# Layer 0's first expert block inside the first stage's plan, and gathered rows turned four blocks at a time by VectorE and SBUF transfers

## Chip, core and metric

The kernel runs on one core of one Trainium2 chip. The metric is the device time of one launch in microseconds (us). Most times below are of one profiled execution; the runs that are compared are timed without a profile.

## What is computed

Two layers work on x of 4 batches x 1024 tokens x 256 features (fp32). Each layer adds a mixing part (layer 0: a form of linear attention; layer 1: a gated feed-forward net with running decay) and a mixture of 8 experts, both behind a layer norm with shifts and scales made from a condition vector. The part that the change touches is layer 0's mixture:

```python
logits = jnp.einsum('bsd,de->bse', input_emb, Wr) + br
route_w = jax.nn.softmax(logits, axis=-1)
_, topk_idx = jax.lax.top_k(route_w, TOP_K)          # 2 of 8 experts for each token
...
h = jax.nn.relu(jnp.einsum('bsd,edh->ebsh', input_emb, W1) + b1[:, None, None, :])
expert_out = jnp.einsum('ebsh,ehd->ebsd', h, W2) + b2[:, None, None, :]
return jnp.einsum('bse,ebsd->bsd', routed, expert_out)
```

with D = 256 features, H = 1024 hidden units, E = 8 experts, and 4096 tokens, so 8192 pairs of token and expert.

## The kernel before

**The first stage** (up to some 115 us of the span) does layer 0's attention part, its layer norms and the routing. Its pieces are given to a planner (`Plan`): each piece has an engine, an estimated time, the pieces it comes after, the buffers it holds and a rank; the planner runs them in a simulated time and so writes down the order of the instructions on each engine. Each engine then works through its own list in that order, and waits on semaphores. The normalised rows are stored to a table in HBM, `h_rows` (L1316), with the token's routing code beside them (L1303).

**The routing's end.** The pairs are sorted by expert into blocks of 128. `total_staged` (PE, L561 and L569) counts pairs, `close_staged` (DVE, L596 to L649) turns the counts into a list of blocks, `across` (PE, L688) spreads it over the partitions, `limits` (DVE, L699 to L714) and `list_weights` (L725 to L736) write the tables. For each block `reach` (DVE, L752), `look` (PE, L765) and `find` (DVE, L778 and L787) find which 128 rows belong to it. Block 0 needs only `begin` (L580 and L583), not the list of blocks. Small matmuls without use (`busy`, L915) keep PE at work in the gaps; PE also makes layer 1's modulation there (`pm_mod`, L1382).

**The expert loop** runs over blocks 0 to 59 (of 71; `turning` = 60) in an order written out by hand. In turn j it issues on POOL the gather of W1 for block j+1 (`weights_in`), the scatter of block j-2's values (`kept`), the gather of W2 for block j (`weights_out`) and the gather of 128 rows of block j+2 (`fetch`); both weight gathers move data only where the expert differs from that of two blocks before. PE does `hidden(j)` (L1698: 16 fp32 matmuls with W1 as weights and the turned rows as moving operand, 2 records each), then turns the rows of block j+1 (`turn_rows`, L1678: two 128x128 transposes into PSUM), looks for block j+3 (L765), and does `values(j-1)` (L1721). ACT adds the bias and rectifies (L1710). DVE copies the turned rows to SBUF (`rows_turned`, L1683), makes the addresses (`aim`, L799), finds the rows, and adds the last bias (L1732). `once(j)` puts 16 loads for layer 1 on the queue of SP, from turn 8 on; SP waits for no block between them.

**The rest.** The last expert blocks (60 to 67) and layer 1 are planned again, in stages that overlap.

The lines to know in the code below: `first_half` and `second_half` plan the first stage, the `for j in range(AHEAD)` loop the first three looks, and the `with tc.manual_schedule(engines=ORDERED | {EngineType.SP})` block is the expert loop.

Of the kernel before, what the change touches and what calls it, by code (L numbers as in the profile page):

```python
# [19 lines left out]
P = 128  # L20
B, S, D = 4, 1024, 256
NC = S // P
KD = D // P
# [9 lines left out]
ROUTER = 64  # L33
STRIP = 32
AHEAD = 3
DX = D + 2
W1ROW = KD * H + KH
W2ROW = KH * D + D
# [101 lines left out]
def adaln_d2_kernel(  # L140
# [218 lines left out]
    class Pairs:  # L359
# [222 lines left out]
            )  # L582
            nc.vector.tensor_copy(self.nth[:, 0:1], lane)  # L583

        def close_staged(self, scratch):


            J, blocks, runs, origin, up1 = self.J, self.blocks, self.runs, self.origin, self.up1
            begin2 = float(J - LATE)

            def t(shape, what, dt=F32):
                return scratch.tile(shape, dt, tag=f"g_{what}", name=f"g_{what}", bufs=1)

# [4 lines left out]
            )  # L598
            blocks_i = t([P, 2, E], "blocks_i", I32)
            nc.vector.tensor_scalar(blocks_i, whole, 7, None, ALU.logical_shift_right)  # L600
            nc.vector.tensor_copy(blocks[:, :, 1:], blocks_i)

            up = t([P, 2, E + 1], "up")
            nc.vector.tensor_tensor_scan(
# [141 lines left out]
        def reach(self, scratch, j):  # L746

            reached = scratch.tile(
                [P, self.halves, P], F16, tag="g_reached", name="g_reached", bufs=3
            )  # L750
            for h in range(self.halves):
                nc.vector.tensor_scalar(  # L752
                    reached[: self.K, h, :],
                    count16[: self.K],
                    self.limit[: self.K, h, j : j + 1],
                    None,
                    ALU.is_ge,
                )
            return reached
# [35 lines left out]
        def aim(self, scratch, xg, j):  # L795


            dest = scratch.tile([P, 1], I32, tag="g_dest", name="g_dest", bufs=8)
            nc.vector.scalar_tensor_tensor(  # L799
                dest,  # L800
                xg[:, D : D + 1],
                self.code[:, j : j + 1],
                xg[:, D + 1 : D + 2],
                ALU.not_equal,
                ALU.add,
            )
            return dest
# [96 lines left out]
    sT1 = silu_of(1, c1)  # L904
    gate_rows = pa.tile([B, 2, D], F32, name="gate_rows", bufs=1)

    plan = Plan(p1=3, p2=2, pm=3, xn1=5, h1T=2, xn2=6, h2T=2, t1=1, le=2)
    PE, ACT, DVE, POOL = "PE", "ACT", "DVE", "POOL"
    tiles = {}
# [299 lines left out]
    def second_half(b):  # L1209
# [73 lines left out]
        for gs in routed:  # L1283
            k, at = 4 * len(gs), 4 * gs[0] * B + b
            tag = (b, gs[0])

            def route(k=k, at=at, tag=tag):
                g0.route(pa, tiles["pl", tag[0], tag[1]][:, :, :E], br_sb, at, k, B)

            d = plan(  # L1290
                DVE,
                0.24 * 14 + 0.16 * 4 if k == NC else 0.22 * 14,
                route,
                after=[ready[g][0] for g in gs],
                holds=[ready[gs[-1]][1]],
                rank=rank - 0.2,
            )
            for g in gs:
                of_batch["route", b, g] = d

            def mark(k=k, at=at):
                first = at - at % B
                nc.sync.dma_start(  # L1303
                    h_rows[first * P : (first + k * B) * P, D:].rearrange(
                        "(c b p) d -> b p c d", b=B, p=P
                    )[at % B],
                    g0.meta[:, at : at + (k - 1) * B + 1 : B, :],
                )

            plan("SP", 1.0, mark, after=[d], rank=rank)  # L1310
            for g in gs:
                back, slot, key = backs[g]

                def store(g=g, key=key):
                    at = 4 * g * B * P
                    nc.sync.dma_start(  # L1316
                        h_rows[at : at + 4 * B * P, :D].rearrange(
                            "(c b p) d -> b p c d", b=B, p=P
                        )[b],
                        tiles["xn", key],  # L1320
                    )

                plan("SP", 4.0, store, after=back, holds=[slot], rank=rank)


    ps = plan.slot("p1")
# [75 lines left out]
        tiles["bases"] = g0.bases(ps_1)  # L1402

    m2 = plan(PE, 0.2, bases, after=[d], holds=[ps2], rank=-1.6)
    d = plan(DVE, 3.9, lambda: g0.close_staged(pa), after=[m], holds=[ps], rank=-1.0)
    bs = plan(
        ACT,
        0.25,
# [3 lines left out]
        rank=-1.6,  # L1412
    )
    begun = plan(DVE, 0.3, g0.begin, after=[bs], rank=-1.6)
    ps = plan.slot("p1")
    m = plan(PE, 0.4, lambda: g0.across(ps_1), after=[d], holds=[ps], rank=-1.0)
    kept_busy(1.1, [m], 30.0)
    d = plan(DVE, 1.4, lambda: g0.limits(pa), after=[m, bs], holds=[ps], rank=-1.0)
    plan(DVE, 1.2, lambda: g0.list_weights(pa), after=[d], holds=[ps], rank=-0.75)
    for j in range(AHEAD):  # L1420
        ps = plan.slot("p1")

        def reach(j=j):
# [8 lines left out]
        first = -1.0 + 0.1 * j if j else -1.6  # L1432
        r = plan(DVE, 0.5, reach, after=[d] if j else [begun], rank=first)
        m = plan(PE, 0.25, look, after=[r], holds=[ps], rank=first)
        plan(DVE, 0.6, find, after=[m], holds=[ps], rank=first if j else -0.95)
        if j < AHEAD - 1:
            kept_busy(0.7, [m], 30.0 + j)
    with tc.manual_schedule(engines=ORDERED):
# [10 lines left out]
    mods1 = [l1.tile([P, B, D], F32, name=f"mod{i}") for i in range(6)]  # L1449
    groups = [Pairs(l1, l1, "ga", 4 * B), Pairs(l1, l1, "gb", 3 * B)]  # L1450
    mod_rows1 = dram.tile([B, 6, D], F32, name="mod_rows1")
    early = ctx.enter_context(tc.tile_pool(name="early", bufs=1))
    poolF = tc.tile_pool(name="poolF", bufs=2, side="right")
    work = poolF.__enter__()
    y0 = dram.tile([2 * B * S, D], F32, name="y0")
    groups_of["g0"], values_of["g0"] = g0, y0

# [23 lines left out]
    RINGS = tuple(room1)  # L1481
    SP = "SP"
    made = {}
    home = {"yg1": early, "h1": early, "hT1": early, "tiny": early}

    def buf(kind, shape):
        return (home[kind] if kind in home else late).tile(
# [184 lines left out]
            ts.append(plan(ACT, 0.67, out_, after=[m], holds=[ps, slotT], rank=rank - 0.03))  # L1672
        return slot, slotT, hs, ts

    def turn_rows(j):
        pt = psum(ps_m, [P, KD, P], "pm_x")
        for k in range(KD):
            nc.tensor.transpose(pt[:, k, :], xgbuf[j % 4][:, k * P : (k + 1) * P], ident)  # L1678
        return pt

    def rows_turned(pt):
        xT = work.tile([P, KD, P], F32, tag="xT", name="xT", bufs=3)
        nc.vector.tensor_copy(xT, pt)  # L1683
        return xT

    def weights_in(j):
        gather(w1buf[j % 2], W1, g0.wrow[:, j : j + 1], E * P - 1)

    def weights_out(j):
        gather(w2buf[j % 2], W2, g0.wrow[:, j : j + 1], E * P - 1)  # L1690

    def hidden(j, xT, m4):
        w1 = w1buf[j % 2]
        p1 = psum(ps_1, [P, 4, P], "p1_h")
        for i in range(4):
            m = 4 * m4 + i
            for k in range(KD):
                nc.tensor.matmul(  # L1698
                    p1[:, i, :],
                    lhsT=w1[:, k * H + m * P : k * H + (m + 1) * P],  # L1700
                    rhs=xT[:, k, :],
                    start=(k == 0),
                    stop=(k == KD - 1),
                )
        return p1

    def rectified(j, hid, p1, m4):
        for i in range(4):
            m = 4 * m4 + i
            nc.scalar.activation(  # L1710
                hid[:, m, :],
                p1[:, i, :],
                AF.Relu,
                bias=w1buf[j % 2][:, KD * H + m : KD * H + m + 1],
            )

    def values(j, hid):
        w2 = w2buf[j % 2]
        p2 = psum(ps_2, [P, D], "p2_y")
        for m in range(KH):  # L1720
            nc.tensor.matmul(  # L1721
                p2,
                lhsT=hid[:, m, :],
                rhs=w2[:, m * D : (m + 1) * D],
                start=(m == 0),
                stop=(m == KH - 1),
            )
        return p2

    def biased(j, p2):  # L1730
        y = work.tile([P, D], F32, tag="y", name="y", bufs=3)
        nc.vector.tensor_tensor(y, p2, w2buf[j % 2][:, KH * D :], ALU.add)  # L1732
        return y

    dests, ys0 = {}, {}

    def aimed(j):
        dests[j] = g0.aim(work, xgbuf[j % 4], j)

    def kept(j):  # L1740
        put("g0", dests[j], ys0[j])

    def new_hidden():
        return work.tile([P, KH, P], F32, tag="hid", name="hid")


    loads = []
    for k in range(KD):
        loads += [(a[:, k, :], w[k * P : (k + 1) * P, :]) for a, w in ((a0, fw0), (a2, fw2))]
# [24 lines left out]
            nc.sync.dma_start(*loads[j - 8])  # L1774

    with tc.manual_schedule(engines=ORDERED | {EngineType.SP}):
        for j in range(2):
            g0.fetch(xgbuf[j], h_rows, j)
        xT, hid = rows_turned(turn_rows(0)), None
        aimed(0)  # L1780
        for j in range(turning):

# [2 lines left out]
                kept(j - 2)  # L1785
            if j:
                weights_out(j)
            g0.fetch(xgbuf[(j + 2) % 4], h_rows, j + 2)
            reached = g0.reach(work, j + AHEAD)
            new = new_hidden()  # L1790
            for m4 in range(2):
                rectified(j, new, hidden(j, xT, m4), m4)

            xT = rows_turned(turn_rows(j + 1))
            aimed(j + 1)
            g0.find(work, g0.look(ps_m, reached), j + AHEAD)
            if j:
                ys0[j - 1] = biased(j - 1, values(j - 1, hid))
            hid = new
            once(j)  # L1800


    plan = Plan(rings=RINGS, **room1)
    of_block = {}

# [762 lines left out]
```

## Time and profile before

| | |
|---|---|
| timed without a profile | 1121.61 us median of 3 runs (1121.43 to 1122.06) |
| the profiled execution: its own time, and its span | 1141.97 us, 1140.2 us |
| PE busy | 1086.3 us, 95% of the span |
| DVE, ACT, POOL busy | 592.0 us, 428.6 us, 422.5 us |
| start of block 0's `hidden`, and of the last matmul of an expert block (67) | 115.0 us, 622.0 us |

How to read the profile: PE is the matmul part of TensorE and PEld its weight loads, which lie beside matmuls; DVE is VectorE, ACT is ScalarE, POOL is GpSimd (it issues gathers), SP is SyncE (it issues plain transfers). A line of the timeline has start, length, engine, source line, operation, tiles written<-read, shapes, and count; what stands in brackets is the idle time ahead of it and what ended it. In a table of stretches each row has the length, the busy time and count of each engine, the granted clock, the mean busy share of the 16 DMA engines, and GB/s.

### The profile page before, as it was taken

To read this page: it belongs to the slowest core of one execution; us is meant where nothing else is said; L and a number is where in the kernel's file an instruction comes from. 1 tells how busy PE (TensorE), PEld (TensorE's weight loads), DVE (VectorE), ACT (ScalarE), POOL (GpSimd) and SP (SyncE) were. 2 spreads that over 40 slices of the span, in tenths; PEclk is the share of its full clock that TensorE was granted. 3 is DMA by queue.
4 is the path that set the end of the run, shared out by engine and by line. 5 is a ranking of instruction groups with operands and counts; after the bars stand their busy time and mean duration, and the time that the engine had idled before them with its cause. 6 is when DMAs were issued, how large, how long until landed. Compare 5 with 4: busy or idle time off the path is not lost. (4 is left out here: it accounts for less than half of the span.)

```text
span 1140.2 us, 18501 instructions
## 1 busy us (share of the span) xinstructions
PE 1086.3 (95%) x6238; PEld 847.0 (74%) x6238; DVE 592.0 (52%) x2308; ACT 428.6 (38%) x1164; POOL 422.5 (37%) x483
## 2 busy tenths in 40 slices
PE   8998999999999999999999999999999999899883
PEld 5894999999999999999988466566576575547641
DVE  7787232222222222222274788975776445888456
ACT  5976333322333323233343343432434235333421
POOL 1000455555555555555543011010044233616452
PEclk8999999999999999999999999999999999999996
DMA  9414549242422415151260312100024223323532
GB/s 321 174 31 103 191 156 302 100 153 75 154 78 75 150 39 192 33 193 40 70 223 27 96 34 83 39 10 19 19 62 129 75 82 103 102 88 107 155 118 93
DMA packets 77693, 122.38 MB, mean 107 GB/s; under 512 B 27340, under 2 KB 57301, under 8 KB 72990
## 3 DMA queue, kind: packets, MB, share of 16 engines
q0 software_dynamic: 31872, 69.68, 19.5%
q1 hardware_dynamic: 44622, 49.92, 13.3%
q10 hardware_dynamic: 1104, 1.58, 0.4%
q8 instruction: 52, 0.85, 0.3%
q14 instruction: 43, 0.35, 0.1%
HBM read 205.25 MB, written 30.22 MB: 207 GB/s over the span
## 5 line engine op out<-in xcount | busy, mean ns | idle before, releaser
L1710 ACT ACTIVATE hid<-p_h,w 128x128 f32<-128x128 f32 x544 | 154.8, 368 | 323.5 <-issue 251.9
L1698 PEld LDWEIGHTS p_h<-xT,w 128*128 128x128 f32 x2176 | 253.2, 192 | 7.2 <-DVE xT L1683 1.9
L1698 PE MATMUL p_h<-xT,w 128*128 128x128 f32 x2176 | 254.7, 275 | 3.1 <-DVE xT L1683 2.7
L1721 PE MATMUL p_y<-w,hid 128*128 128x256 f32 x1088 | 249.0, 382 | 0.2 <-issue 0.2
L2007 PE MATMUL p_u<-hT,a 128*128 128x512 f32 x512 | 232.0, 596 | 2.9 <-ACT hf L2019 1.4
L1721 PEld LDWEIGHTS p_y<-w,hid 128*128 128x128 f32 x1088 | 201.6, 190 | 25.1 <-DMA w<-in_W,g_wrow 0.4
L2007 PEld LDWEIGHTS p_u<-hT,a 128*128 128x128 f32 x512 | 93.5, 190 | 100.5 <-issue 89.7
L347 POOL DMA_INDIRECT w<-in_W,g_wrow x134 | 135.1, 1008 | 77.4 <-ACT hid L1710 46.7
L1683 DVE COPY xT<-pm_x 128x256 f32<-128x256 f32 x68 | 28.8, 424 | 187.0 <-PE pm_x L1678 134.4
L812 POOL DMA_INDIRECT y<-y,g_dest x68 | 69.5, 1022 | 143.5 <-DVE g_reached L752 108.4
L2055 PE MATMUL p_f<-a,hf 128*128 128x256 f32 x512 | 116.7, 380 | 2.0 <-DVE step L2096 1.0
L1732 DVE TENSOR_TENSOR y<-p_y,w 128x256 f32<-128x256 f32 x68 | 28.9, 425 | 166.9 <-PE p_y L1721 160.7
L2055 PEld LDWEIGHTS p_f<-a,hf 128*128 128x128 f32 x512 | 95.9, 190 | 20.8 <-issue 5.9
L347 POOL DMA_INDIRECT xg<-h_rows,g_row x68 | 66.7, 980 | 120.4 <-DVE g_row L787 98.9
L2103 POOL TENSOR_TENSOR x_sb<-x_sb,step 128x256 f32<-128x256 f32 x32 | 24.9, 778 | 205.8 <-DVE step L2096 153.6
L2315 PE MATMUL p_e<-ew,xT 128*128 x280 | 71.5, 386 | 0.8 <-ACT y L2325 0.8
L2019 ACT ACTIVATE hf<-p_u,decay 128x512 f32<-128x512 f32 x56 | 38.2, 685 | 74.9 <-PE p_u L2007 63.5
L347 POOL DMA_INDIRECT xg<-ga_rows,ga_row x39 | 37.3, 956 | 54.1 <-DVE g_hits L778 19.3
L2315 PEld LDWEIGHTS p_e<-ew,xT 128*128 128x128 f32 x280 | 49.0, 190 | 11.0 <-issue 3.8
L2023 DVE SCALAR_TENSOR_TENSOR hf<-p_u,decay,hf 128x512 f32<-128x512 f32 x56 | 41.9, 748 | 25.7 <-PE p_u L2007 14.3
L1618 DVE TENSOR_TENSOR h<-h,mod 128x256 f32<-128x256 f32 x128 | 51.6, 425 | 6.8 <-ACT h L1608 4.1
L2325 ACT COPY y<-p_e 128x256 f32<-128x256 f32 x70 | 26.1, 373 | 51.4 <-PE p_e L2315 19.2
(371 smaller groups left out, 1259.1 us busy)
## 6 DMA issues: line engine op xcount, KB each, us to landing
yg<-y SPq DMA_DIRECT2D x32, 256.0 KB
ga_y<-y SPq DMA_DIRECT2D x39, 128.0 KB
x_sb<-in_x SPq DMA_DIRECT2D x8, 512.0 KB
h_rows<-xn SPq DMA_DIRECT2D x8, 512.0 KB
gb_y<-y SPq DMA_DIRECT2D x31, 128.0 KB
out_x<-x_sb SPq DMA_DIRECT2D x7, 512.0 KB
a<-in_fw SPq DMA_DIRECT2D x6, 512.0 KB
mod<-mod_rows SPq DMA_DIRECT2D x6, 512.0 KB
```

The source lines that it names most:

```text
L347: return nc.gpsimd.indirect_dma_start(out=dst, out_offset=None, in_=table, in_offset=bass.IndirectOffsetOnAxis(ap=index, axis=0), bounds_c ...
L812: nc.gpsimd.indirect_dma_start(out=table, out_offset=bass.IndirectOffsetOnAxis(ap=dest, axis=0), in_=y, in_offset=None, bounds_check=2 * s ...
L1618: nc.vector.tensor_tensor(h, h, mods1[(sc, sh)[i]][:, b, :], (ALU.mult, ALU.add)[i])
L1698: nc.tensor.matmul(p1[:, i, :], lhsT=w1[:, k * H + m * P : k * H + (m + 1) * P], rhs=xT[:, k, :], start=(k == 0), stop=(k == KD - 1),)
L1710: nc.scalar.activation(hid[:, m, :], p1[:, i, :], AF.Relu, bias=w1buf[j % 2][:, KD * H + m : KD * H + m + 1],)
L1721: nc.tensor.matmul(p2, lhsT=hid[:, m, :], rhs=w2[:, m * D : (m + 1) * D], start=(m == 0), stop=(m == KH - 1),)
L1732: nc.vector.tensor_tensor(y, p2, w2buf[j % 2][:, KH * D :], ALU.add)
L2007: nc.tensor.matmul(pu, lhsT=a[:, k, m * P : (m + 1) * P], rhs=made["n1", c, "hT"][:, k, :, :], start=(k == 0), stop=(k == KD - 1),)
L2019: nc.scalar.activation(made[key, m], made[key, m, 0], AF.Silu, scale=decays[c])
L2023: nc.vector.scalar_tensor_tensor(h, made[key, m, 1], decays[c], h, ALU.mult, ALU.mult)
L2055: nc.tensor.matmul(made[key, "p2", b], lhsT=made[key, m][:, b * P : (b + 1) * P], rhs=a1[:, m, :], start=(m == 0), stop=(m == KH - 1),)
L2315: nc.tensor.matmul(made[key, "p2"], lhsT=made[key, "xT"][:, k, :], rhs=ew_flat[:, bass.ds(made[key, "at"] + k * D, D)], start=(k == 0), st ...
```

## The change

It has two parts.

1. Block 0's row gather, turning, `hidden` and `values` become pieces of the first stage's plan (`first_block`), and the copy of its turned rows is done by ACT. The first three instructions of `close_staged` become `whole_blocks`; the rest of it, `across`, `limits` and `list_weights` are entered in the plan after block 0's look and find. Block 1's gather is planned too.
2. Blocks 12 to 59 come in groups of four (a quad). Their rows are gathered up to eight blocks ahead into a buffer of four blocks (`xgquad`). At the end of turn j (j = 8, 12, ..., 52) `quad_turned(j + 4)` has DVE turn 32x32 squares, two instructions of 128x512 values, and SP issue 16 transfers from SBUF to SBUF of 32 partitions x 256 values, which put the squares in their places. The moving operand of `hidden` is then four runs of 32 columns that lie 256 values apart. PE's two transposes and DVE's copy are gone for these 48 blocks. The looks run up to ten blocks ahead, two in each of turns 2 to 8. W1's rows are laid out differently by the host, so the rows are turned with a step of two; for blocks 0 to 11 and 60 to 67 this step is in the weight load of PE's transposes. The buffers `early` for the start of layer 1 are taken after the loop, in place of the quads' buffers.

```diff
-            dest = scratch.tile([P, 1], I32, tag="g_dest", name="g_dest", bufs=8)
+            dest = scratch.tile([P, 1], I32, tag="g_dest", name="g_dest", bufs=16)
...
-    d = plan(DVE, 3.9, lambda: g0.close_staged(pa), after=[m], holds=[ps], rank=-1.0)
+    whole = plan(DVE, 0.45, lambda: g0.whole_blocks(pa), after=[m], holds=[ps], rank=-1.0)
...
+    def quad_turned(j):
+        rows = xgquad[j // QUAD % 2]
+        square = quads.tile([P, P // SQ, KD, QUAD, SQ], F32, tag="square", name="square", bufs=1)
+        for k in range(KD):
+            nc.vector.transpose(
+                square[:, :, k, :, :].rearrange("p m b s -> p b m s"),
+                rows[:, :, k:D:KD].rearrange("p b (m f) -> p b m f", f=SQ),
+            )
+        xT = quads.tile([P, P // SQ, KD, QUAD, SQ], F32, tag="xTq", name="xTq")
+        for q in range(P // SQ):
+            for m in range(P // SQ):
+                nc.sync.dma_start(
+                    xT[m * SQ : (m + 1) * SQ, q, :, :, :], square[q * SQ : (q + 1) * SQ, m, :, :, :]
+                )
+        for b in range(QUAD):
+            turned_quads[j + b] = [xT[:, :, k, b, :] for k in range(KD)]
+            dests[j + b] = g0.aim(work, rows[:, b, :], j + b)
...
+    def first_block(found):
+        slots = [plan.slot("xn1") for _ in range(2)]
+        kept0 = tiles["first"] = {}
+        rows = plan(
+            POOL, 1.0, lambda: g0.fetch(xgbuf[0], h_rows, 0), after=[found, *stores], rank=-1.6, lag=1.9
+        )
...
+        m = plan(PE, 0.35, turn, after=[rows], holds=[ps, *slots], rank=-1.5)
+        h = plan(ACT, 0.45, lambda: nc.scalar.copy(kept0["xT"], kept0["pt"]), after=[m], holds=[ps, *slots], rank=-1.5)
...
     for j in range(AHEAD):
+        if j == 1:
+            closed = plan(
+                DVE, 3.5, lambda: g0.close_staged(pa), after=[whole, found], rank=-1.0
+            )
...
-        plan(DVE, 0.6, find, after=[m], holds=[ps], rank=first if j else -0.95)
+        found = plan(DVE, 0.6, find, after=[m], holds=[ps], rank=first)
+        if j == 0:
+            first_block(found)
...
-        for j in range(2):
-            g0.fetch(xgbuf[j], h_rows, j)
-        xT, hid = rows_turned(turn_rows(0)), None
+        looks = {0: (3,), 1: (4,)} | {j: (j + 3, j + 10) for j in range(2, 9)}
+        fetches = {j: (j + 2,) for j in range(4)} | {j: (j + 2, j + 8) for j in range(4, 10)}
+        xT, hid = None, None
...
-            xT = rows_turned(turn_rows(j + 1))
-            aimed(j + 1)
-            g0.find(work, g0.look(ps_m, reached), j + AHEAD)
-            if j:
+            if in_quads(j + 1):
+                xT = turned_quads.pop(j + 1)
+            else:
+                xT = rows_turned(turn_rows(j + 1))
+                aimed(j + 1)
+            for r, hit in zip(sought, reached):
+                g0.find(work, g0.look(ps_m, hit), r)
+            if j == 1:
+                ys0[0] = biased(0, tiles["first"]["p2"])
+            elif j:
                 ys0[j - 1] = biased(j - 1, values(j - 1, hid))
+            if j % QUAD == 0 and in_quads(j + QUAD):
+                quad_turned(j + QUAD)
```

## The prediction

> **What bounds the kernel now.** I read the page first, for who is busy and when; then the table of stretches, for the stages apart; then the timeline of PE inside one turn of the expert loop, and of PE and DVE where the first stage ends.
>
> ```profile
> span 1140.2 us, 18501 instructions
> ...
> PE 1086.3 (95%) x6238; PEld 847.0 (74%) x6238; DVE 592.0 (52%) x2308; ACT 428.6 (38%) x1164; POOL 422.5 (37%) x483
> ```
>
> ```profile
> 241.84:249.25 7.41, 7.41 (x55) 6.99 (x53) 1.73 (x8) 2.28 (x8) 3.99 (x5) 1.00 0.54 179
> 115.00:560.00 445.00, 444.59 (x3131) 419.32 (x3132) 109.29 (x503) 139.10 (x485) 238.65 (x239) 1.00 0.38 125
> 650.00:1140.00 490.00, 452.62 (x1802) 281.26 (x1800) 341.54 (x1235) 171.22 (x412) 145.61 (x158) 0.98 0.26 78
> ```
>
> Of the 445 us of the loop PE is without work for 0.41 us, at full clock. DVE has work for a quarter of it, POOL for a little over half. So a microsecond taken from PE's list in the loop is a microsecond off the span, and DVE, ACT, POOL and the DMA engines (0.38 busy) have room.
>
> One turn of the loop on PE:
>
> ```profile
> 245.68 3.73 PE L1698 MATMUL p_h<-xT,w 128*128 128x128 f32 x32
> 249.25 0.38 PE L1678 MATMUL pm_x<-ident,xg 128*128 128x128 f32 x2
> 249.47 0.28 PE L765 MATMUL pm_counts<-g_more,g_reached 128*128 128x129 f16 x2
> 249.59 3.67 PE L1721 MATMUL p_y<-w,hid 128*128 128x256 f32 x16
> 253.09 3.73 PE L1698 MATMUL p_h<-xT,w 128*128 128x128 f32 x32
> ```
>
> From start to start a turn takes 253.09 - 245.68 = 7.41 us. The lengths overlap, as matmuls are pipelined; what a group costs is the distance to the next start: `hidden` 3.57, the two transposes 249.47 - 249.25 = 0.22, the look 0.12, `values` 3.50.
>
> The end of the first stage:
>
> ```profile
> 105.26 1.02 PE L1382 MATMUL pm_mod<-wmod,sT 128*4 128x512 f32 x2
> 106.22 0.29 PE L765 MATMUL pm_counts<-g_more,g_reached 128*128 128x129 f16 x2
> ...
> 109.82 0.48 PE L688 MATMUL pm_blocks<-g_diagonal,ones 128*128 128x142 f32 x2 [1.61 <-DVE g_filled L649]
> ...
> 113.47 0.43 PE L1678 MATMUL pm_x<-ident,xg 128*128 128x128 f32 x2
> 115.01 3.81 PE L1698 MATMUL p_h<-xT,w 128*128 128x128 f32 x32 [1.10 <-DVE xT L1683]
> 118.65 0.38 PE L1678 MATMUL pm_x<-ident,xg 128*128 128x128 f32 x2
> ```
>
> Here a chain on DVE sets the pace: `across` at 109.82 waits for `close_staged`, and the first `hidden` waits for its turned rows.
>
> **What the Trainium skill says.** "TensorE: Matmul & The Clock Gate", Part 4 (PE-mode transpose), gives about 275 ns for a transpose in a kernel. The records agree (mean 273 ns), but the distance to the next start is 0.11 us, and only that is saved. "Vector Engine (DVE) Microarchitecture Reference", 3.8 (the reshape front-end), has DVE's 32x32 transpose sustain one element per cycle and lane; no run here shows it. "SBUF - State Buffer", SBUF: two separate sides, says that reads stay at full rate while accesses hit the same line of 16 bytes, four fp32 values; runs of 32 values would then cost nothing. The nearest row here agrees as far as it goes: the dense experts of layer 1 (L2363) read two runs of 256 values, and four of their records take 1.72 us, as do four of L2007 with one run of 512. "DMA: Bandwidth & Descriptors", Why small descriptors are slow, exempts SBUF to SBUF; the trace has no such transfer.
>
> **Part 2, the quads.**
> - Removed from PE: in 48 turns two transposes, 48 x 0.22 = 10.5 us, all on the bounding engine. I count nothing for the wait in front of the next matmul, as 48 more weight loads of the same sort follow.
> - Looks: 63 in the loop before and after, only earlier: 0.
> - `hidden` with four runs of 32 columns: unknown. Below: 0, as nothing makes it faster. Above: 1536 records (48 x 32) that are now 0.112 us apart. I take 0, for the two reasons above, and because a 128-column pass alone would need about 0.108 us (half of the 0.216 us between two 256-column records of L1721), so 4 ns of a slower read would hide. The upper end goes to the first rival.
> - Each quad's first `hidden` waits on eight transfer semaphores and a gather. Satisfied waits cost nothing visible: the first L2055 record, which has eleven in the built order, starts 0.429 us after the record ahead of it, the usual distance.
> - DVE, per quad: two 128x512 squares at 0.68 us (nearest row: a 128x512 TENSOR_TENSOR, L1231, 675 ns) and four `aim` at 0.21, 2.2 us; gone are four copies at 0.42 and the same `aim`. At worst, four times 0.68 each, it is 6.3 us inside one turn of 7.2 us that had 1.7 us of DVE work; behind it on DVE stand the next turn's reach, and find and the bias at its end. So 0, and if that cover were gone up to 0.8 us x 12 = 10 us. Behind those in turn waits only POOL's scatter, two turns later.
> - SP, per quad: 16 transfers of 32 KB. The built order has each wait for the eighth before it, so two landings in sequence. With 0.36 us to issue one (the 8 KB L1303 entry) and 2.5 us to land (xg issued at 110.48, last packets at 113): 16 x 0.36 + 2 x 2.5 = 11 us, after 2.2 us on DVE; the rows are read three turns, 21.6 us, after they are started. Cover of 8 us; 0.
> - DMA engines: a quad is 512 KB in 1 KB packets, like one `h_rows` store, which moved at some 330 GB/s: 1.6 us of all engines per 29 us. The loads for layer 1 on SP now stand behind the quads of turns 8 to 20 and so come in fours (2 MB) after each, in place of one burst around 160 to 190 us. A weight gather (1.05 MB, by its packets mostly 3.4 to 4.3 us, even the one inside that burst) landed 1.7 us or more before its matmul in the loop, most of them 3.2 to 4.5. 0.
> - POOL: the same number of gathers, each fetch earlier than needed. 0. Steps of two in the weight load of 20 blocks' transposes: two values in each line of 16 bytes, 0 to 0.1 us each; I take 0.
>
> **Part 1, block 0.** The built order of PE decides: block 0's `hidden` and `values` are not in a gap; they stand behind both other looks and the last `busy`, where turn 0 stood. What moves is the chain in front. Look 0 now stands behind two pieces of `pm_mod` (0.94 each, from 105.26): 107.15 instead of 106.22. On DVE find 0 is now ahead of the rest of `close_staged`: its result is out at 107.15 + 0.29 + 0.14 + 0.54 = 108.12, and `close_staged` goes on then, not at 106.68: 1.44 us later. The row gather leaves two us earlier, but nobody uses that: `across`, the looks and `busy` come first, all 1.44 us late, so the transposes start at 114.91. ACT's copy (0.38) in place of a DVE that was still at `list_weights` gives `hidden` a start 1.0 us after them, not 1.54: 115.92, 0.9 us later than before. Then `values(0)` follows at once, and so no longer covers the wait for block 2's turned rows: pm_x to p_h takes 0.90 (118.65 to 119.55) twice, where the second time it was 0.33 of work followed by `values`: 0.57 lost. Sum: +1.45 us at the start of block 2's `hidden`, with the same work done. Bounds: 0 (the planner's spare time in `busy` gives way) to 2.5.
>
> **Sum.** -10.5 + 1.45 = -9.1 us. The span of 1140.2 becomes 1131.1, the profiled execution 1141.97 becomes 1132.9. The median of the timed runs lies 20.4 us under the profiled execution; where they differ the trace can't say, but a loop that is bound by PE at full clock should take the same in both. So 1121.61 - 9.1 = 1112.5. What comes next is then `hidden` and `values` themselves, 7.19 us a turn; after 560 us layer 1 follows in the same order on PE, only earlier.
>
> **Rivals.**
> 1. *Slower: the broken-up moving operand.* Place: L1475 in the changed kernel, blocks 12 to 59. Price: a cost at each of the four jumps of a record; it decides from 9.1 / 1536 = 5.9 ns per record on, that is records over 118 ns apart. At 4 ns a jump, 16 a record less the 4 that hide, 12 x 1536 = 18.4: net +9.3, 1131. For: no row here has runs so short. Against: L2363 shows no cost for its jump.
> 2. *Contention eats a part.* The fours of loads and a quad meet weight gathers (turns 9, 13, 17, 21; by their packets, 9 and 17 have such gathers): at 1.5 us for each of four, +6: 1118.5. For: DMA share there was already 0.5 to 0.8. Against: spare time that is mostly over 3 us, and a gather of 4.3 us within a burst at full rate.
> 3. *The change frees nothing* because the squares or transfers arrive late and PE stands for what it saved: 0.8 us a quad, some 1121.6. Against: 8 us of cover.
>
> **Chances.** The likeliest 0.75 (its own range 1110 to 1115.5: part 1 between 0 and +2.5, and 0.2 us a turn either way of small terms), rival 2 0.09, rival 3 0.05, rival 1 0.11. About 0.2% (2.2 us) is what a measurement of this kernel can tell from no change: faster 0.84, same 0.05, slower 0.11. The range reaches through rival 2: 1110 to 1119.
>
> **What would show it.** In the changed kernel's profile: no L1427 records in the loop after block 11, turns of 7.19 us, p_h records still 0.112 us apart, no PE wait on a transfer; StreamTranspose at 0.6 to 0.7 us; the first `hidden` at about 115.9 and block 2's at about 128.5 (127.07 before). Records over 0.118 us apart, or idle time of PE ahead of a quad's first `hidden`, would make me wrong.

## The result, and the profile after

Timed without a profile the changed kernel takes 1112.03 us (median of 4 runs, 1110.79 to 1114.69), the kernel before, on the same chip, 1121.52 (4 runs, 1120.87 to 1122.06): a ratio of 0.9925, 95% interval 0.9913 to 0.9938, so 7.0 to 9.8 us less. The forecast was 1112.5.

The profiled execution of the changed kernel took 1110.79 us. That of the kernel before (1141.97) was an odd one: the run `e1_before_again` profiles the same kernel with a span of 1120.6 us, the same times up to block 60 within 2 us, and 21.5 us less in layer 1. So nothing below is read from the difference of two spans; each part is measured from PE's own starts.

The first two rows of the page of the changed kernel that matter, the span and the busy time of the engines:

```profile
span 1109.1 us, 18511 instructions
...
PE 1065.2 (96%) x6142; PEld 835.1 (75%) x6142; DVE 588.0 (53%) x2283; ACT 430.0 (39%) x1165; POOL 423.4 (38%) x483
```

The table of stretches, with the same columns as before (length, busy time and count of PE, PEld, DVE, ACT, POOL, then clock, DMA share, GB/s), for one turn and for the loop:

```profile
241.00:248.19 7.19, 7.19 (x52) 6.76 (x52) 3.06 (x13) 2.29 (x8) 4.01 (x4) 1.00 0.68 211
115.00:550.00 435.00, 431.07 (x3006) 405.13 (x3005) 105.56 (x480) 138.79 (x482) 237.34 (x237) 1.00 0.44 142
```

A turn is 7.19 us. But the loop, in which PE stood idle for 0.41 us before, now has 3.93 us without work. PE in one turn, by its timeline:

```profile
321.33 3.73 PE L1475 MATMUL p_h<-xTq,w 128*128 128x128 f32 x32
324.90 0.28 PE L772 MATMUL pm_counts<-g_more,g_reached 128*128 128x129 f16 x2
325.02 3.67 PE L1499 MATMUL p_y<-w,hid 128*128 128x256 f32 x16
328.52 3.73 PE L1475 MATMUL p_h<-xTq,w 128*128 128x128 f32 x32
```

The transposes are gone from between `hidden` (L1475) and the look (L772), and the rest kept its place: 3.57, 0.12, 3.50. The end of the first stage, by PE's timeline:

```profile
105.65 0.29 PE L772 MATMUL pm_counts<-g_more,g_reached 128*128 128x129 f16 x2
105.78 0.81 PE L923 MATMUL pm_busy<-busy 128*128 128x512 f16 x3
109.57 0.48 PE L695 MATMUL pm_blocks<-g_diagonal,ones 128*128 128x142 f32 x2 [2.99 <-DVE g_filled L656]
109.89 1.96 PE L923 MATMUL pm_busy<-busy 128*128 128x512 f16 x5
...
114.68 3.84 PE L1475 MATMUL p_h<-xn,w 128*128 128x128 f32 x32 [0.46 <-ACT xn L1543]
118.35 3.62 PE L1499 MATMUL p_y<-w,xn 128*128 128x256 f32 x16
121.81 0.39 PE L1427 MATMUL pm_x<-ident,xg 128*128 128x128 f32 x2
122.86 0.28 PE L772 MATMUL pm_counts<-g_more,g_reached 128*128 128x129 f16 x2 [0.66 <-PE pm_x L1427]
123.20 3.84 PE L1475 MATMUL p_h<-xT,w 128*128 128x128 f32 x32
```

Block 0's `hidden` and `values` stand one behind the other (114.68 and 118.35), ahead of the loop. `across` (L695) waits for 2.99 us, where it was 1.61, and block 3's look for 0.66 us.

All kernels of this study, cut at four starts on PE: the first `pm_turn` matmul of the routing (L450 before), block 2's `hidden`, block 60's, and layer 1's first `p_u` matmul; us, from the trace of each. The ratio is to the kernel before, timed on the same chip (1120.95 to 1122.76 us there, by chip). An instruction that the trace lists is called a record.

| kernel | timed ratio to before, 95% | routing to block 2 | block 2 to 60 | block 60 to layer 1 | layer 1 to the end |
|---|---|---|---|---|---|
| before | | 26.37 | 430.19 | 67.80 | 515.19 |
| the change | 0.9925 (0.9913 to 0.9938) | 28.52 | 423.04 | 65.18 | 493.05 |
| e1_before_again | 0.9995 (0.9983 to 1.0006) | 27.99 | 430.58 | 67.63 | 493.69 |
| e2_quads_only | 0.9900 (0.9881 to 0.9919) | 26.41 | 424.99 | 65.17 | 494.35 |
| e3_block0_only | 1.0026 (1.0017 to 1.0035) | 27.91 | 431.87 | 67.43 | 494.88 |
| e4_loads_ahead | 0.9893 (0.9873 to 0.9914) | 28.80 | 420.40 | 65.07 | 494.42 |
| e5_quads_loads | 0.9884 (0.9869 to 0.9898) | 26.39 | 420.24 | 65.15 | 494.51 |
| e6_step4 | 1.1496 (1.1481 to 1.1511) | 28.77 | 600.36 | 65.46 | 494.33 |
| e7_late_fetch | 0.9887 (0.9869 to 0.9904) | 26.39 | 419.81 | 65.97 | 494.48 |
| e8_step_two | 1.0015 (1.0008 to 1.0021) | 28.26 | 431.35 | 67.80 | 496.16 |
| e9_before_shifted | 0.9991 (0.9983 to 0.9999) | 26.35 | 430.19 | 64.96 | 495.18 |
| e10_quads_shifted | 0.9906 (0.9892 to 0.9920) | 26.38 | 420.38 | 67.95 | 494.17 |
| e11_step2 | 0.9955 (0.9942 to 0.9967) | 27.89 | 424.89 | 66.02 | 493.51 |

In the row of the change each of three columns has something that the forecast did not have: the loop gained 7 us and not 10, and the blocks after it gained 2.5 us where the forecast saw nothing to gain. The experiments go after these.

### The profile page after: what moved, and what is told of

The parts are those of the page before. It is cut to its first block, busy times and chain, and to the rows that moved or that the text cites. A ratio compares the mean times of both kernels' runs of the same rounds, so it can differ in the third digit from the quotient of the medians.

```text
span 1109.1 us, 18511 instructions
## 1 busy us (share of the span) xinstructions
PE 1065.2 (96%) x6142; PEld 835.1 (75%) x6142; DVE 588.0 (53%) x2283; ACT 430.0 (39%) x1165; POOL 423.4 (38%) x483
## 4 chain that ended last, share of the span: by engine, by line
PE 81%; DVE 8%; DMA 6%; ACT 2%; issue 2%; POOL 0%; SPq 0%; ACTq 0%; DVEq 0%; POOLq 0%
PE p_h L1475 20%; PE p_y L1499 20%; PE p_u L2127 19%; PE p_f L2175 10%; PE p_e L2435 4%; DMA w<-in_W,g_wrow 4%; PE pm_x L2418 1%; DVE ln_st L984 1%; PE pm_t L1838 1%; DMA xg<-gb_rows,gb_row 1%; PE pm_counts L772 1%; ACT h2T L1055 1%; ACT xn L1010 1%; DVE ln_mv L985 1%; DVE step L2508 1%
## 5 line engine op out<-in xcount | busy, mean ns | idle before, releaser
L1499 PE MATMUL p_y<-w,hid 128*128 128x256 f32 x1072 | 245.0, 382 | 2.8 <-DMA w<-in_W,g_wrow 2.8
L1499 PEld LDWEIGHTS p_y<-w,hid 128*128 128x128 f32 x1072 | 198.7, 190 | 27.6 <-DMA w<-in_W,g_wrow 3.3
L1475 PEld LDWEIGHTS p_h<-xTq,w 128*128 128x128 f32 x1536 | 179.1, 192 | 2.5
L1475 PE MATMUL p_h<-xTq,w 128*128 128x128 f32 x1536 | 179.2, 275 | 0.0
L785 DVE TENSOR_SCALAR_CACHE_REDUCE g_hits<-pm_counts,g_nth 128x128 f16<-128x128 f32 x68 | 23.6, 348 | 105.2 <-PE pm_counts L772 105.1
L1475 PE MATMUL p_h<-xT,w 128*128 128x128 f32 x608 | 71.4, 276 | 0.5 <-DVE xT L1432 0.4
L1475 PEld LDWEIGHTS p_h<-xT,w 128*128 128x128 f32 x608 | 70.3, 192 | 1.4 <-DVE xT L1432 0.8
L349 POOL DMA_INDIRECT xg<-h_rows,g_row x20 | 19.8, 990 | 107.7 <-DVE g_own L636 97.1
```

Source lines behind the costliest of these rows:

```text
L349: return nc.gpsimd.indirect_dma_start(out=dst, out_offset=None, in_=table, in_offset=bass.IndirectOffsetOnAxis(ap=index, axis=0), bounds_c ...
L1475: nc.tensor.matmul(p1[:, i, :], lhsT=w1[:, k * H + m * P : k * H + (m + 1) * P], rhs=xT[k], start=(k == 0), stop=(k == KD - 1),)
L1499: nc.tensor.matmul(p2, lhsT=hid[:, m, :], rhs=w2[:, m * D : (m + 1) * D], start=(m == 0), stop=(m == KH - 1),)
```

## The experiments

**The kernel before once more, and each part alone.** `e1_before_again` has no edit.

> The kernel before, unchanged, for a second profile. The first profiled execution took 20 us longer than the median of the timed runs, so its last stages are no fair baseline. Both theories: 1121.5 us within 0.2%; the loop's turns 7.41 us as before; the profiled execution near 1122, with the time that is missing against the first profile taken from layer 1 (first p_u to the end about 495 us, not 515).

It sets the scale: 1122.15 us, and a span of 1120.6. Its 27.99 in the first column is 1.6 us over the 26.37 of the first trace, because block 0's 32 `p_h` records ran with the granted clock at half for 3.4 us. The same lies in `e8_step_two` (28.26), and in no other trace of a kernel with block 0 in its old place.

`e2_quads_only` takes part 1 back:

```diff
-    whole = plan(DVE, 0.45, lambda: g0.whole_blocks(pa), after=[m], holds=[ps], rank=-1.0)
+    d = plan(
+        DVE,
+        3.9,
+        lambda: (g0.whole_blocks(pa), g0.close_staged(pa)),
+        after=[m],
+        holds=[ps],
+        rank=-1.0,
+    )
...
-        if j == 0:
-            first_block(found)
...
-        xT, hid = None, None
+        for j in range(2):
+            g0.fetch(xgbuf[j], h_rows, j)
+        xT, hid = rows_turned(turn_rows(0)), None
```

> The quads alone; block 0 stays in the loop as before. Theory 1 (the quads give 48 x 0.22 = 10.5 us and lose about 3.5 us to W2 gathers that come late; planning block 0 early costs 1.5 to 2.2 us): 1121.5 - 10.5 + 3.5 = 1114.5 by the loop alone, and faster than the full change by 1.5 to 2.2 us on the same chip. Theory 2 (the full change's 9.5 us is more than the loop's net 7.1, so planning block 0 early brings the other 2 us): slower than the full change by 2 us or more.

`e3_block0_only` takes the quads back; the rows are still turned with the step of two, in all blocks:

```diff
-        return 3 * QUAD <= j < turning
+        return False
...
-        looks = {0: (3,), 1: (4,)} | {j: (j + 3, j + 10) for j in range(2, 9)}
-        fetches = {j: (j + 2,) for j in range(4)} | {j: (j + 2, j + 8) for j in range(4, 10)}
+        looks = {j: (j + AHEAD,) for j in range(turning)}
+        fetches = {j: (j + 2,) for j in range(turning)}
```

> Block 0 planned early alone; no quads, looks and fetches as before (rows still turned with a step of two, by TensorE). Theory 1: slower than before by 1.5 to 2.2 us, about 1123.3, and block 2's hidden starts that much later after the first pm_turn. Theory 2: faster than before by 2 us or more, 1119.5 or less. Turns of the loop 7.41 us in both; a step of two in the transposes' weight load would show as longer turns.

The kernel before took 1122.65 us on their chip. The quads alone take 1111.74 us, part 1 alone (with the step of two in all blocks, priced below) 1125.37: the gain is the quads', and part 1 costs. (The 1114.5 us expected of the quads alone lacked the gain after the loop, on which more below.) Where PE kept its clock, the first column is 26.35 to 26.41 without part 1 (before, `e2`, `e5`, `e7`, `e9`, `e10`) and 27.89 to 27.91 with it (`e3`, `e11`): +1.5 us, where the forecast had +1.45. In the change, `e4` and `e6` it is 28.5 to 28.8: behind the 3 us of idle time at `across` the granted clock fell to half until about 114 to 115 us, and `busy` and the looks took longer (five `busy` records 1.96 us, 1.24 before).

**Weight gathers that come late.** The waits of PE in the loop of the change, by what they waited for (us in total, times, longest), and in its timeline the second of them, the 1.12 us ahead of block 19's `values`:

```profile
PE p_y L1499 <- DMA w<-in_W,g_wrow: 2.8, 3, 1.5
```

```profile
265.64 0.28 PE L772 MATMUL pm_counts<-g_more,g_reached 128*128 128x129 f16 x2
267.04 3.72 PE L1499 MATMUL p_y<-w,hid 128*128 128x256 f32 x16 [1.12 <-DMA w<-in_W,g_wrow]
```

Before there was no such wait. SP's timeline of the change shows what shares the DMA engines with these gathers:

```profile
182.69 11.18 SPq L1455 DMA_DIRECT2D xTq<-square  x16
193.91 2.22 SPq L1880 DMA_DIRECT2D a<-in_fw  x4
213.72 11.24 SPq L1455 DMA_DIRECT2D xTq<-square  x16
225.00 1.13 SPq L1880 DMA_DIRECT2D a<-in_fw  x2
226.18 1.05 SPq L1880 DMA_DIRECT2D mod<-mod_rows  x2
242.53 11.78 SPq L1455 DMA_DIRECT2D xTq<-square  x16
254.36 2.87 SPq L1880 DMA_DIRECT2D mod<-mod_rows  x4
```

A quad keeps SP for 10.3 to 11.8 us, the loads for layer 1 stand behind it and go out in fours at its end (193.91, 254.36), and meet the W2 gathers of the next turns. By the packets, that of block 19 (261.67 to 266.49) starts to move 4.6 us after its issue on POOL, where 1.7 is usual: the loads' packets are ahead of it. The first wait, 1.53 us ahead of block 11's `values`, comes behind the loads of 193.91 in the same way (4.2 us from issue to first packet); the third, 0.16 us, behind a quad's own transfers. `e4_loads_ahead` is the whole change with all 16 loads in turn 7, ahead of the first quad:

```diff
-        if 8 <= j < 8 + len(loads):
-            nc.sync.dma_start(*loads[j - 8])
+        if j == 7:
+            for dst, src in loads:
+                nc.sync.dma_start(dst, src)
```

> The full change, with layer 1's 16 loads issued in one go in turn 7, ahead of the first quad on SP's queue. Theory 1 (two of the three late W2 gathers, at blocks 12 and 20, meet the loads that stand behind a quad): those two waits go, 1.75 + 1.34 us, and the one at block 27, which meets a quad's own transfers, stays: 1109. Rival (the quads' transfers alone make the gathers late): no change, 1112.

1110.89 us, by the ratios 3.6 us under the change, though the intervals just overlap. Of the waits on W2 in its loop one is left:

```profile
PE p_y L1499 <- DMA w<-in_W,g_wrow: 0.2, 1, 0.2
```

(The recorded text counts by turns: the `values` of blocks 11, 19 and 26 stand in turns 12, 20 and 27.) The loop takes 420.40 us in place of 423.04: the price of the late gathers is 2.6 us. What went is the late start: the first packets of both gathers move 1.7 us after issue again. How long the packets then take is not what decides: 5.8 and 5.4 us here, 5.6 and 4.8 in the change, 3.6 to 3.9 in the kernel before (but for one of 5.6). In `e2_quads_only` it was more than its waits: two of 3.4 us in sum, and after the longer one (1.93 us, behind a quad's first `hidden`) 16 `values` records took 5.41 us in place of 3.7, at half the clock.

`e5_quads_loads` has both edits, the quads alone (as `e2`) and the loads in turn 7 (as `e4`).

> Part 2 alone (block 0 stays where it was), and the 16 loads for layer 1 are all issued in turn 7, ahead of the first quad on SP, as in the run e4_loads_ahead. If what the runs so far show adds up (the quads 10.5 us less on PE, late blocks 2.5 less, step of two in 20 blocks' transposes 0.4 more, no matmul late by a weight gather), it takes 12.6 us less than the kernel before: a ratio of 0.989, under the change itself, since part 1 costs 1.5 to 2 us and the late W2 gathers 2.6 to 3.4. If part 1 gains something that its stage's table doesn't show, it is no better than e4_loads_ahead (ratio 0.9893), and if the late gathers were chance, no better than e2_quads_only (0.9900). In the trace: from the first transposes to block 2's hidden 26.4 us, the loop some 421.5 us, no PE wait on a gather of W2.

1109.37 us (1109.12 to 1109.68), without a wait of PE on a gather over 0.15 us in the loop. With `e7_late_fetch`, a variant of it below, it is the fastest kernel here, and its interval lies below that of the change. Against `e4` the ratios overlap; part 1's 1.5 us are in the traces, not in the comparison of these two.

**The step of two in the transposes' weight load.** `e8_step_two` is the kernel before with W1's layout and the slice `k:D:KD` of the change, in all 68 blocks:

```diff
-            nc.tensor.transpose(pt[:, k, :], xgbuf[j % 4][:, k * P : (k + 1) * P], ident)
+            nc.tensor.transpose(pt[:, k, :], xgbuf[j % 4][:, k:D:KD], ident)
```

> The kernel before with nothing changed but W1's layout and, with it, the step of two values in the weight load of the transposes, in all 68 blocks. The forecast put this at 0 (up to 0.1 us a block, for 20 blocks). By e3_block0_only the weight load takes 200 ns in place of 142 and a turn 0.022 us more: 1.5 us in all, a ratio of 1.0013, and the loop 431.7 us in place of 430.4. If e3's slower turns came from its other part, the loop stays at 430.4 us and the ratio is 1.000.

1123.88 us. The two forms of the weight load in its trace, layer 1's with neighbours (L2298) and layer 0's with the step (L1678); ns at least, median, most:

```profile
L2298 PEld LDWEIGHTS pm_x<-ident,xg x140: 137/141/145, 847.3 to 1077.7; 128*128 128x128 f32 x140
...
L1678 PEld LDWEIGHTS pm_x<-ident,xg x136: 194/202/222, 114.3 to 611.2; 128*128 128x128 f32 x136
```

60 ns more in the load, of which 0.02 us reach the turn (7.433 in place of 7.413): 1.2 us from block 2 to 60. So `e3_block0_only` holds both this and part 1, 1.0026 against 1.0015, and in the change, with 20 such blocks, it is 0.4 us.

**The moving operand.** The forecast hung on this cost more than on any other, and set it at nothing. `e6_step4` keeps all bytes and instructions of the change, but lays the squares out with the block innermost, so that a block's 128 columns lie four values apart:

```diff
-        square = quads.tile([P, P // SQ, KD, QUAD, SQ], F32, tag="square", name="square", bufs=1)
+        square = quads.tile([P, P // SQ, KD, SQ, QUAD], F32, tag="square", name="square", bufs=1)
...
-            turned_quads[j + b] = [xT[:, :, k, b, :] for k in range(KD)]
+            turned_quads[j + b] = [xT[:, :, k, :, b] for k in range(KD)]
```

> The whole change, but the squares are laid out so that each block's 128 columns lie four values (16 bytes) apart in the moving operand, in place of four runs of 32 neighbours; bytes and instructions are the same. It tests the price that the forecast set to nothing, and the first rival. If the moving operand has room for slower reads, or reading by lines of 16 bytes doesn't matter at this rate, records stay 0.112 us apart and the time stays at that of the change (1112). If every value in its own line costs what a step of two costs in the weight load (60 ns for 128 values), 1536 records cost 92 us: about 1204. Decided by the distance of the p_h records in blocks 12 to 59.

1290.89 us: neither figure, far over both. One `hidden` in its timeline, and what follows it:

```profile
402.78 7.52 PE L1475 MATMUL p_h<-xTq,w 128*128 128x128 f32 x32
410.12 0.30 PE L772 MATMUL pm_counts<-g_more,g_reached 128*128 128x129 f16 x2
```

32 records take 410.12 - 402.78 = 7.34 us, 0.229 each in place of 0.112, so 0.117 x 1536 = 180 us: the whole loss (the loop is 177 us longer than the change's, as in these longer turns no gather is late). `e11_step2` lies between, with a step of two values:

```diff
-        xT = quads.tile([P, P // SQ, KD, QUAD, SQ], F32, tag="xTq", name="xTq")
+        xT = quads.tile([P, P // SQ, KD, 2, SQ, 2], F32, tag="xTq", name="xTq")
...
-            turned_quads[j + b] = [xT[:, :, k, b, :] for k in range(KD)]
+            turned_quads[j + b] = [xT[:, :, k, b // 2, :, b % 2] for k in range(KD)]
```

> The whole change, but in xTq each block's 128 columns lie two values (8 bytes) apart, between the runs of 32 neighbours of the change and the step of four values of e6_step4, where p_h records were 0.229 us apart. DVE has four squares of 128x256 for a quad in place of two of 128x512. If the moving operand is read by lines of 16 bytes at the rate that e6 shows (128 lines in 0.229 us, so 64 lines in 0.114), records are 0.112 to 0.115 us apart, and the time is 1112 to 1116. If any step but one halves the rate, they are 0.229 apart, and it takes about 1290 as e6.

1116.87 us, 0.9 over the range expected.

```profile
401.40 3.79 PE L1476 MATMUL p_h<-xTq,w 128*128 128x128 f32 x32
405.03 0.28 PE L772 MATMUL pm_counts<-g_more,g_reached 128*128 128x129 f16 x2
```

Its 32 records take 3.63 us, 0.1134 each, and a turn is 7.25 us in place of 7.19: 2.7 us in 48 turns. (The loop is only 1.9 us longer than the change's, as it waits 0.7 us less for W2 gathers; 0.8 more lie between block 60 and layer 1.) A rate of 1.79 ns for each line of 16 bytes (0.229 / 128) gives 0.1145 for 64 lines, within 1% of what was measured. At 32 lines, the change itself, it would be 0.057 and lies under the 0.112 that the pass takes anyway. So a rate by lines fits all three layouts; no run looks inside the read. This agrees with the Trainium skill, "SBUF — State Buffer", SBUF: two separate sides, which has full rate from two hits in a line. For the weight load it doesn't: there a step of two already costs 60 ns.

**The 2.5 us after the loop.** From block 60 to layer 1 each kernel with quads takes 65.1 to 66.0 us (but for `e10`, which comes last), and before, `e1`, `e3` and `e8` 67.4 to 67.8. In `e1_before_again`'s timeline PE waits there twice for turned rows:

```profile
583.24 3.84 PE L1698 MATMUL p_h<-xT,w 128*128 128x128 f32 x32 [1.49 <-DVE xT L1683]
591.64 3.84 PE L1698 MATMUL p_h<-xT,w 128*128 128x128 f32 x32 [0.77 <-DVE xT L1683]
```

DVE's copies for blocks 63 and 64 stand behind layer 1's first combining of values, which waits for SP's reads of them (`yg`), which wait for the scatter of block 59's values. In `e1` the first read goes out 1.1 us ahead of block 62's `hidden`, in those kernels with quads 2.5 to 2.7 us ahead. The first theory was that in those no row gathers lie beside that scatter. `e7_late_fetch` is `e5` with the last two where they were before:

```diff
         fetches = {j: (j + 2,) for j in range(4)} | {j: (j + 2, j + 8) for j in range(4, 10)}
+        fetches |= {j: () for j in range(52, 58)} | {58: (60,), 59: (61,)}
```

> As e5_quads_loads, but the rows of blocks 60 and 61 are gathered in turns 58 and 59, as in the kernel before, in place of turns 52 and 53. It asks where the 2.4 us in the late blocks (60 to 67) come from that every kernel with quads saves. Theory: without row gathers in the last turns the scatter of block 59's values lands sooner, so SP's first reads of them for layer 1 go out before block 62's hidden and ahead of a W1 gather; then here the scatter has a row gather beside it again, those reads go out about a us later against block 62, PE waits for the turned rows of blocks 63 and 64, and from block 60's hidden to layer 1's first matmul it takes 67.4 us and not 65.1: 2.3 us more than e5. Rival: another thing that the quads change (DVE's free time, layer 1's buffers) makes the difference, and it stays at 65.1 us.

The theory fell: the first read still leaves 2.7 us ahead, and the time is 1109.23 us. (0.8 us came back elsewhere: `yg`'s fourth part was late.) The packets then showed another thing. From the records of the trace, us after the scatter's issue on POOL (the scatter has 32 packets of 4096 bytes):

```
                    30th packet  16 KB instruction  last packet  first read of yg
                    starts       packet starts      ends         issued
before                 2.62           2.96             4.59          5.17
e1_before_again        3.63           3.75             5.37          5.95
e3_block0_only         3.61           3.72             5.35          5.93
e8_step_two            3.74           3.89             5.52          6.10
the change             3.44           none             3.78          4.51
e2_quads_only          3.47           none             3.72          4.44
e5_quads_loads         3.45           none             3.73          4.47
e7_late_fetch          3.41           none             3.69          4.42
```

Where an instruction packet (0.95 us long) lies among the scatter's, the last two packets are 1.6 us later, and with them everything that waits. In the loop such packets come every 18 us on average, in which PE has some 250 records (matmuls and weight loads: 252 in `e1`, 253 in the change). The Trainium skill, "Trainium Architecture — The Big Picture", The software stack, gives an instruction 64 bytes, so 16 KB are 256. The two counts suggest that the packets bring PE's instructions; then the number of records of PE ahead decides where they fall, and that can be tested. `e9_before_shifted` adds 44 records at the start of the kernel before, `e10_quads_shifted` 182 at the start of `e5`, with matmuls without use that are narrower and more:

```diff
-    plan(PE, 6.5, lambda: busy(5.0), holds=[ps], at=0.5, rank=-5.0)
+    plan(PE, 6.5, lambda: busy(5.0, 2 * P), holds=[ps], at=0.5, rank=-5.0)
```

(98 columns in place of `2 * P` in the second.)

> The kernel before with one edit: the matmuls without use at its very start are 45 of 256 columns and not 23 of 512, the same time with 44 more records of PE (22 matmuls, 22 weight loads). It tests what makes the 2.4 us in blocks 60 to 67 that every kernel with quads saves. Theory: PE's instructions are fetched in packets of 16 KB, one for some 256 records; in the kernels without quads one such packet lies between those of the scatter of block 59's values (1.1 us after most of them, on the way of the last two), which so land 2 us later, and layer 1's first reads wait for them. 44 records more bring that fetch about 3 us earlier, ahead of the scatter: then from the scatter's issue to the first read it takes 4.5 us and not 5.2 to 6.1, the read goes out 2.6 us ahead of block 62's hidden and not 1.1, and from block 60's hidden to layer 1's first matmul it takes 65.2 us and not 67.6: 2.4 us less than the kernel before, a ratio of 0.998. Rival: the quads themselves (DVE's free time, buffers) make the difference, and all this stays as it was.

> The opposite of e9_before_shifted: the fastest kernel so far (e5_quads_loads), with 114 narrower matmuls without use at the start in place of 23, so 182 more records of PE, which by the count of records should bring an instruction fetch to where it lies in the kernels without quads, 3.3 us ahead of block 62's hidden, among the packets of the scatter. Theory: then two of the scatter's packets land 2 us late, and from block 60's hidden to layer 1's first matmul it takes 67.5 us and not 65.15; 2.4 us more than e5_quads_loads. Rival: no change, 65.15. If the fetch misses the scatter, which the packets tell, it says nothing.

Both ways it went as the theory has it. In `e9` no instruction packet is left beside the scatter: last packet after 3.92 us, first read after 4.35, 2.67 ahead of block 62, and 64.96 us from block 60 to layer 1, though not one quad is in this kernel. In `e10` the packet lies there (3.70), the last of the scatter ends after 5.33, the read goes out after 6.22, and block 60 to layer 1 takes 67.95. In all thirteen traces it goes with the packet: 67.4 to 68.0 us in the five that have one there, 65.0 to 66.0 in the eight that have none. The DMA view of that stretch (queue, kind: packets, MB, share of the engines), and PE's timeline:

```profile
q0 software_dynamic: 419, 1.34, 54.8%
q8 instruction: 1, 0.02, 0.8%
```

```profile
572.68 3.84 PE L1487 MATMUL p_h<-xT,w 128*128 128x128 f32 x32 [1.67 <-DVE xT L1444]
```

The timed sizes are 1111.68 us for `e10` (0.9906 against 0.9884 of `e5`: 2.5 us, about as expected, though the intervals touch) and 1119.95 for `e9` (0.1 to 1.9 us less than before, where 2.4 was expected; in its profiled execution layer 1 took 1.5 us longer than in `e1`, within what that column of the table varies by). That the fetch in `e9` moved by 10 us and not by 3 was not expected either. That a fetch and the two late packets share one of the 16 DMA engines is argued; the trace does not name the engine.

## Why the prediction was right

The total was right, with its largest term and the zero that it hung on; the smaller terms that it lacked or set at nothing nearly cancel. That they do is luck: `e4` takes the late gathers away and `e10` the 2.5 us after the loop, each without touching the rest.

- *Removed from PE, 10.5 us.* Right: turns of 7.19 us, as foretold, and no wait for a quad's transfers ahead of a `hidden`. (The sign "no PE wait on a transfer" did not hold: PE waited 2.8 us for W2 gathers, see below.)
- *The broken-up moving operand, 0* (rival 1). Right for the change. The two reasons given, a line of 16 bytes that is used whole and a pass that hides slower reads, fit the three layouts. But the bound was set at four jumps of 4 ns a record; `e6` shows that the danger was the step within a run, not the jump, and how large: 0.117 us a record.
- *DVE, the quads' squares at 0.68 us.* Right: 0.686. The trace of the change has the two of a quad in 1.29 us and the four `aim` in 0.57, so 1.9 in place of 2.2:

```profile
L1448 DVE STREAM_TRANSPOSE square<-xq x24: 668/686/714, 181.3 to 502.5; 128x512 f32<-128x512 f32 x24
```

- *SP, 11 us a quad.* 10.3 to 11.8 us, but by another sum: an issue takes 0.589 us (median), not 0.36, and the next follows 0.63 us after it; the landings lie mostly inside. The cover of 8 us held, and PE waits for no quad.
- *DMA engines, 0.* This step failed. The loads in fours did delay weight gathers: 2.6 us, by `e4`. Rival 2 had the mechanism and at 1.5 us a meeting (measured 1.53 and 1.12), about the price, but four meetings in turns 9, 13, 17 and 21; two cost anything to speak of. The places were wrong because the loads were taken to go out with the quad, while they stand 11 us behind its start (the forecast's own figure for SP), and so meet the gathers of turn 11 and turns 18 and 19; and the spare time of 3.2 to 4.5 us was read off a loop in which this burst came at another place.
- *The step of two, "0 to 0.1 us each; I take 0".* Wrong in the value taken, within the bounds: 0.022 us each, 0.4 in all.
- *Part 1, +1.45.* +1.5 where the clock holds, so right, by two errors that cancel. `hidden(0)` came 0.4 us earlier than worked out (14.80 us after the first `pm_turn` in `e3`, 15.22 in the forecast), and its turned rows for block 1 took 1.39 us, not 0.90: block 3's look was put behind them without a wait, but waited 0.66 us. Another 0.6 to 0.9 us came from the clock, in three of five traces with part 1. (From the span's start both marks, 115.9 and 128.5, came earlier, 114.68 and 127.79, but the first `pm_turn` itself came 1.43 us earlier in this trace.)
- *The looks, 63 before and after; layer 1 "in the same order, only earlier".* Wrong by omission: the 2.5 us after the loop are in no step. They belong to the number of instructions ahead of them.

In sum: -10.5 + 0.4 + 2.6 + 1.5 - 2.5 = -8.5, and -7.8 with the clock's share; measured -7.0 to -9.8.

## What to carry to other kernels

Cost an operand's layout by the values used of each line of 16 bytes, not by the number of its runs: for this moving operand four were free, two nearly, one doubled the pass; and give weight loads their own price. When work is put on a queue, ask what stands behind it there and when that now goes out: the loads for layer 1 were untouched by the diff's aim, and cost 2.6 of the 10.5 us until they were issued ahead. And before a change of 2 us is put down to its mechanism, shift the instruction stream once: here an instruction packet among those of a scatter that the next stage waits for cost 2.5 us.

## What the runs showed of the hardware

- A 16 KB instruction packet, one for some 250 records of PE, takes a place among the data packets; beside a scatter of 32 packets the last two were 1.6 us late.
- A moving operand of 128 fp32 columns at a step of 16 bytes passes in 0.229 us, at 8 bytes in 0.1134, in runs of 32 neighbours in 0.112. DVE's 32x32 transposes write slower at a step of 16 bytes too: 1.094 us for 128x512, 0.686 with neighbours.
- A weight load of 128x128 fp32 for a transpose takes 141 ns, 202 ns at a step of two (`e8`).
- Behind SP's loads a gather from POOL moved its first packet 4.2 and 4.6 us after its issue (the change), 1.7 us without them (`e4`).
- After 3 us without work PE's granted clock fell to half for about 3.4 us in three traces of five; in `e2` after a wait of 1.93 us, and at block 0's `hidden`, after 1.1 us or less, in two of eight traces of kernels with block 0 in its old place. In `e4` and `e6` it fell at 97.5 and 98.1 us too, where no wait in the 6 us ahead is over 0.65 us. Which waits do it is open.
